# A graph layer on one core: the sums of a round in one stretch, the second layer behind the places, the loop cut ahead of the turns

## The chip, the cores and the metric

The kernel runs on one core of one Trainium2 chip. The metric is the device time of one execution in microseconds (us). About 0.3%, 0.8 us, is what repeated runs can tell from no change.

## The reference

A pre-normalised graph layer with a residual: node features are normalised over their 128 columns, edge features are summed into the node at the edge's end, and a two-layer perceptron is applied to both. There are 12,500 nodes with 128 features, 412,500 edges with 48 features, sorted by their end `dst`; the global vector is one for all nodes, so it is only a bias.

```python
h = jnp.maximum(_layernorm(x, axis=-1), 0.0)
agg = segment_sum(edge_attr_48, dst, num_segments=12500)      # 412500 x 48 -> 12500 x 48
u = graph_globals[zeros]                                      # one row of 64 for all nodes
hid = relu(concatenate([h, agg, u], axis=1) @ W1 + b1)        # 240 -> 256
x = x + hid @ W2 + b2                                         # 256 -> 128
```

All is float32.

## The kernel before

**Rounds.** A loop of 12 rounds handles 1024 nodes and 33,792 edges each; an epilogue does the rest. The nodes of a round are two blocks, A and B, of 512 (128 partitions by 4). The edges of a round are 11 groups of 3072, kept in six *slots*: slots 0 to 3 and 5 hold two groups, slot 4 holds one. A group is loaded as one transfer of 576 KB on SP's queue, for the next round as soon as this round's sums of its slot are done; slots have one buffer each.

**Sums.** Since edges are sorted, a chunk of 768 edges ends in few nodes. `fetch` copies the relative ends of this round's edges from the table `rel` to `rel_i` (L672); `onehots` (VectorE, L686) compares them with a ramp of 28, which makes one-hot matrices `oh`; `sums` (TensorE, L739) multiplies them with the edges, 24 small matmuls a group, into one of two PSUM banks S0 and S1 in turn, and ScalarE copies the result to `ss` (L743). A float32 matmul appears as two records in the profile, so slots 0 to 2 are 288 records and slots 3 to 5 are 240.

**Places.** `places` (VectorE, L692, L705) makes one-hot windows `pl` of 186 nodes, `place` and `place_ends` (TensorE, L761, L726) put the summed chunks at their nodes' columns, in PSUM banks `ax` and `ay`; `sums_out` (ScalarE, L804) copies these to `ags`.

**Normalisation.** `stats` (L768), `variance` (L773 to L778), the root on ScalarE (L779), `shift` (L784, L785) and `norm` (ScalarE, L789, four instructions a block) make `xn` of both blocks. `turn` (L798) transposes it on TensorE, and ScalarE copies it to `ht` (L799).

**Layers.** `layer_x` (L808) and `layer_e` (L813) add the two parts of the first layer in four PSUM banks (PH0 and PH1, PT and PO), each for one block and one half of the hidden 256; `relu` (ScalarE, L818) writes `hid`. The second layer of a round (`second`, TensorE, L834, 16 records a block) is done in the round after, into PH0 and PH1; VectorE adds `xb`, which is x plus the bias, and holds the result in SBUF (L838); `add_b` (L793) makes the `xb` of the new round. Then x of the next round may be loaded, on ScalarE's queue. The held results are stored after the loop.

**Order.** Every engine runs its own instructions in the order in which `body` names them, so an instruction that waits holds back all that is behind it on its engine, the loads on ScalarE's and SP's queues too. `Flow` works out the semaphores. TensorE's loop is cut at another place than that of the other engines: it runs from the operation named in `f.mark` round to the one before it, with one more trip, and the part ahead of the mark on the first trip is skipped. At first trip, where there is no second layer to do, `f.brief` gives one tiny matmul in its place. TensorE's start (the transposes of `dst`, one sum) stands inside this loop, after the first part.

In TensorE's order a round before is: sums 0, 1, 2; second layer of A and of B; sums 3, 4, 5; turns A, B; places; x layer; edge layer. The mark is `su3`, the sums of slot 3.

Of the kernel before, what the change touches and what calls it, by code (L numbers as in the profile page):

```python
# [18 lines left out]
P = 128  # L19
# [35 lines left out]
class Flow:  # L55
# [139 lines left out]
    def run(self):  # L195
# [53 lines left out]
        with nc.Fori(0, hi - lo + 2, 1, engines=[nc.tensor.engine]) as j:  # L249
            with nc.tensor.If(j > 0):  # L250
                for o in own[cut:]:
                    repeat(o, None)
                count("PE")
            with nc.tensor.If(j < 1):
                self.straight([o for o in start if o["eng"] == "PE"])
                ahead("PE")
            with nc.tensor.If(j < hi - lo + 1):
                for brief, some in groupby(own[:cut], lambda o: o["name"] in self.brief):
                    some = list(some)
                    if not brief:  # L260
                        for o in some:
                            repeat(o, None)
                        continue
                    with nc.tensor.If(j > 0):
                        for o in some:
                            repeat(o, None)
                    with nc.tensor.Else():
                        for o in some:
                            repeat(dict(o, emit=self.brief[o["name"]]), None)
        self.straight(end)  # L270
# [151 lines left out]
def kernel(  # L422
# [73 lines left out]
    ot = [const.tile([P, r, D], F32, name=f"ot{k}") for k, r in two]  # L496
    st = [const.tile([P, r, 6], F32, name=f"st{k}") for k, r in two]
    sm = [const.tile([P, 4, r], F32, name=f"sm{k}") for k, r in two]
    sc = [const.tile([P, r], F32, name=f"sc{k}") for k, r in two]
    sh = [const.tile([P, r], F32, name=f"sh{k}") for k, r in two]  # L500

# [107 lines left out]
    def dst_2(b):  # L609
# [4 lines left out]
        dv = df[b % DF].rearrange("c (p t) -> c t p", t=T)  # L614
        rv = rel[:, b * P * T:(b * P + rows) * T].rearrange("p (c t) -> p t c", t=T)
        for t0 in range(0, T, 3):
# [47 lines left out]
    def fetch(j):  # L664

        it = (f.at or 0) + j
        g0, g1 = it * GI + 1, min(NG, (it + 1) * GI + 1)
        m = GI * CG
        blocks = [b for b in range(NB) if b * P < g1 * CG and (b + 1) * P > g0 * CG]
        rv = rel_i.rearrange("p g t -> p (g t)")  # L670

        op("DVE", "fr", ["relz"] + [f"rel{b}.{t0}" for b in blocks for t0 in (0, 3)], ["rel_i"], lambda i: [nc.vector.tensor_scalar(  # L672
            rv, cols(rel, i, lambda i: ((i + j) * GI + 1) * q, m * T), 0.0, None, OP.add)])

# [92 lines left out]
    def stats(k, m=P):  # L767
        op("DVE", f"st{k}", [f"x{k}", f"x{k}t"], [f"st{k}"], lambda i: [nc.vector.bn_stats(st[k][:m, r], xt[k][:m, r]) for r in range(RR[k])])  # L768

    def variance(k, m=P):  # L770
        s = sm[k][:m]
        op("DVE", f"sm{k}.0", [f"st{k}"], [f"sm{k}a"], lambda i: [
            nc.vector.tensor_tensor(s[:, 0:2], st[k][:m, :, 1:3].rearrange("p r c -> p c r"), st[k][:m, :, 4:6].rearrange("p r c -> p c r"), OP.add)])  # L773
        op("DVE", f"sm{k}.1", [f"st{k}"], [f"sm{k}b"], lambda i: [
            nc.vector.tensor_tensor(s[:, 2], st[k][:m, :, 1], st[k][:m, :, 4], OP.subtract)])
        f.chain("DVE", f"sm{k}.2", [f"sm{k}a"], [f"sm{k}b"],
            lambda: nc.vector.tensor_tensor(s[:, 2], s[:, 2], s[:, 2], OP.mult),
            lambda: nc.vector.scalar_tensor_tensor(s[:, 3], s[:, 2], D / 4.0, s[:, 1], OP.mult, OP.add))  # L778
        op("ACT", f"sq{k}", [f"sm{k}b", "eps"], [f"sc{k}"], lambda i: [nc.scalar.activation(sc[k][:m], s[:, 3], AF.Sqrt, bias=eps[:m], scale=1.0 / D)])  # L779

    def shift(k, m=P):
        s = sm[k][:m]
        f.chain("DVE", f"sh{k}", [f"sm{k}a"], [f"sc{k}", f"sh{k}"],
            lambda: nc.vector.reciprocal(sc[k][:m], sc[k][:m]),  # L784
            lambda: nc.vector.scalar_tensor_tensor(sh[k][:m], s[:, 0], -0.5, sc[k][:m], OP.mult, OP.mult))  # L785

    def norm(k, m=P):
        op("ACT", f"xn{k}", [f"x{k}", f"x{k}t", f"sc{k}", f"sh{k}"], [f"xn{k}"], lambda i: [
            nc.scalar.activation(xn[k][:m, r], xt[k][:m, r], AF.Relu, bias=sh[k][:m, r:r + 1], scale=sc[k][:m, r:r + 1]) for r in range(RR[k])])  # L789

# [38 lines left out]

    def second(k, m=P, bk=None, key="PO", keep=None):  # L830

        ov = (po if bk is None else bk)[:, :RR[k] * D].rearrange("p (r d) -> p r d", r=RR[k])
        op("PE", f"w2{k}", [f"hid{k}.{a}" for a in range(NH)] + ["w2"], [key], lambda i: [
            nc.tensor.matmul(ov[:m, r], hid[k][:, a, r, :m], w2[:, a], start=(a == 0), stop=(a == NH - 1)) for r in range(RR[k]) for a in range(NH)])  # L834
        if keep is None:
# [10 lines left out]
    def prologue():  # L846
# [30 lines left out]
        dma("POOL", "lb2", [], ["b2"], b2_sb, b2[None, :].to_broadcast([P, D]))  # L877
        pool("relz", ["relz"], lambda: nc.gpsimd.memset(rel[:, NCH * T:], 0.0))

# [22 lines left out]
        onehot(5, oh[5][:, q:], ["rel0.0", "rel0.3"], rel[:, :q].rearrange("p (g t) -> p g t", g=1))  # L902
        op("PE", "su5", ["oh5", "e5.1"], ["S1"], lambda i: [
# [21 lines left out]
        split("plf", plf, far_, ["off0"], lambda j: off[:, 0:1])  # L925
        op("DVE", "f0", ["rel0.0", "rel0.3"], ["farm"], lambda i: [nc.vector.tensor_reduce(farm, rel[:, :q], AX.X, OP.max, apply_absolute_value=True)])

    def body(it):
        f.at = it

        def add_slots(*some):
            for s in some:
                sums(s)
                if it < NIT - 1:
                    load_e(s, 1)

        keep = lambda i: (i + NIT - 2) % (NIT - 1)
        farthest()
        fetch(1)
        add_slots(0, 1)  # L940
# [36 lines left out]
        layers(layer_e)  # L977
        layers(relu)

    def epilogue():  # L980
# [5 lines left out]
        stats(Z, m)  # L986
        variance(Z, m)
        shift(Z, m)
        norm(Z, m)
# [41 lines left out]
    f.order((0, NIT - 1))  # L1031
    f.mark = "su3"
    f.brief = {f"w2{k}": lambda i, k=k: [nc.tensor.matmul(ph[k][:, 0:1], hid[k][:, 0, 0], w2[:, 0, 0:1], start=True, stop=True)] for k in (A, B)}
    tc.mark_branch_hint_location("skip", engines=[ET.PE, ET.DVE])
# [35 lines left out]
```

## Time and profile before

| | |
|---|---|
| median of 3 runs | 261.3 us (260.92 to 261.72) |
| profiled execution | 261.09 us, span of its instructions 259.3 us |
| TensorE busy | 237.5 us, 92% |
| VectorE busy | 237.4 us, 92% |
| ScalarE busy | 128.6 us, 50% |
| transfers | 94.33 MB, mean 364 GB/s |

The profile is of one execution. Busy time is the time in which an engine had at least one instruction under way. In lists of instructions, L739 is a line of the kernel, `s<-e,oh` is what it writes and reads, x288 is how many follow each other; PE is TensorE, PEld its weight load, DVE VectorE, ACT ScalarE, SP the engine that issues most transfers; a q behind an engine is its queue of issues. In the page's slices the span is cut into 40 equal parts, a digit is a share in tenths. "issue" as the cause of a stop means that the engine waited for nothing that the profile shows.

### The profile page before, as it was taken

What the parts mean: (1) busy time and instruction counts of PE and PEld (TensorE: products, weight loads), DVE (VectorE), ACT (ScalarE), POOL (GpSimd) and SP (SyncE); (2) the same over time, 40 slices, a digit from 0 to 9 for tenths busy, and PEclk for the clock granted to TensorE, in tenths of its full rate; (3) what the DMA queues carried; (4) which work ended last, traced back from release to release, by engine and by line L of the source; (5) the groups of instructions that cost most, each with busy time, mean ns of one, the idle gap of its engine ahead of it and who ended that gap; (6) DMA issues with size and microseconds to landing.
All of it is one profiled execution on the core that took longest, in us unless ns stands there. A gap on an engine that the chain in (4) does not pass through costs nothing.

```text
span 259.3 us, 17135 instructions
## 1 busy us (share of the span) xinstructions
PE 237.5 (92%) x7539; PEld 185.9 (72%) x7540; DVE 237.4 (92%) x643; ACT 128.6 (50%) x326; POOL 9.1 (4%) x23
## 2 busy tenths in 40 slices
PE   0864889999999999999999999999999999999990
PEld 0854765976967958949859769679589498597680
DVE  5799999999999999999999999999999999999640
ACT  4630454644645536646546446455366465564520
POOL 8200020000000000000000000000000000000000
PEclk9997599999999999999999999999999999999999
DMA  6999999999999999999999999999999999959951
GB/s 215 285 380 388 364 389 391 390 392 390 390 392 390 391 392 390 391 392 390 390 393 390 393 389 391 392 385 388 393 382 389 393 385 390 393 210 350 364 223 65
DMA packets 79012, 94.33 MB, mean 364 GB/s; under 512 B 3227, under 2 KB 72189, under 8 KB 78998
## 3 DMA queue, kind: packets, MB, share of 16 engines
q1 hardware_dynamic: 75398, 87.63, 94.6%
q10 hardware_dynamic: 3312, 6.03, 6.1%
q0 software_dynamic: 288, 0.49, 0.7%
q8 instruction: 7, 0.11, 0.2%
q14 instruction: 7, 0.06, 0.1%
HBM read 87.75 MB, written 6.40 MB: 363 GB/s over the span
## 4 chain that ended last, share of the span: by engine, by line
PE 86%; DVE 6%; DMA 2%; issue 2%; ACT 1%; SPq 0%; DVEq 0%
PE s L739 26%; PE ph L834 17%; PE ph L808 9%; PE ax L761 7%; PE ph L813 5%; PE po L808 4%; PE pt L808 4%; PE pt L813 4%; DVE oh L686 3%; PE pt L798 3%; DMA holda<-in_dst_dram 2%; PE po L798 2%; PE ax L726 2%; DVE pl L692 1%; PE s L992 1%
## 5 line engine op out<-in xcount | busy, mean ns | idle before, releaser
L686 DVE TENSOR_TENSOR oh<-iota_v,rel_i 128x1344 f32<-128x1344 f32 (+1 forms) x78 | 108.6, 1435 | 0.0
L739 PEld LDWEIGHTS s<-e,oh 128*28 128x28 f32 x6336 | 73.0, 110 | 18.3 <-issue 15.9
L739 PE MATMUL s<-e,oh 128*28 128x48 f32 x6336 | 76.9, 211 | 8.1 <-issue 4.6
L743 ACT COPY ss<-s 128x96 f32<-128x96 f32 (+1 forms) x72 | 16.5, 230 | 26.6 <-PE s L739 26.5
L692 DVE TENSOR_SCALAR pl<-iota_w,off_i 128x186 f32<-128x186 f32 x117 | 27.6, 312 | 0.4
L789 ACT ACTIVATE xna<-xa,sha,sca 128x128 f32<-128x128 f32 x48 | 19.8, 482 | 15.9 <-DVE sha L785 15.9
L818 ACT ACTIVATE hida<-ph,bias 128x512 f32<-128x512 f32 x12 | 8.2, 687 | 38.3 <-PE ph L813 38.3
L834 PE MATMUL ph<-w,hida 128*128 128x128 f32 x192 | 24.6, 281 | 0.0
L834 PE MATMUL ph<-w,hidb 128*128 128x128 f32 x192 | 23.4, 275 | 0.0
L834 PEld LDWEIGHTS ph<-w,hida 128*128 128x128 f32 x192 | 22.3, 191 | 0.8
L834 PEld LDWEIGHTS ph<-w,hidb 128*128 128x128 f32 x192 | 22.4, 192 | 0.0
L789 ACT ACTIVATE xnb<-xb,shb,scb 128x128 f32<-128x128 f32 x48 | 19.6, 480 | 0.0
L761 PE MATMUL ax<-pl,ss 128*48 128x186 f32 (+1 forms) x120 | 19.4, 309 | 0.0
L761 PE MATMUL ay<-pl,ss 128*48 128x186 f32 (+1 forms) x120 | 19.4, 309 | 0.0
L761 PEld LDWEIGHTS ax<-pl,ss 128*48 128x48 f32 x120 | 13.8, 123 | 4.7 <-issue 2.0
L799 ACT COPY hta<-pt 128x512 f32<-128x512 f32 x12 | 7.0, 587 | 15.2 <-DVE xbb L793 14.9
L761 PEld LDWEIGHTS ay<-pl,ss 128*48 128x48 f32 x120 | 13.8, 123 | 0.0
L813 PE MATMUL ph<-ags,w1a 48*128 48x512 f32 x48 | 13.5, 641 | 0.0
L808 PE MATMUL ph<-hta,w1h 128*128 128x512 f32 x24 | 13.5, 645 | 0.0
L808 PE MATMUL ph<-htb,w1h 128*128 128x512 f32 x24 | 12.3, 592 | 0.0
L808 PE MATMUL pt<-hta,w1h 128*128 128x512 f32 x24 | 12.3, 592 | 0.0
L808 PE MATMUL po<-htb,w1h 128*128 128x512 f32 x24 | 12.3, 592 | 0.0
(162 smaller groups left out, 334.7 us busy)
## 6 DMA issues: line engine op xcount, KB each, us to landing
e<-in_edge_attr_dram SPq DMA_DIRECT2D x133, 576.0 KB, 9.3
xa<-in_x_dram ACTq DMA_DIRECT2D x11, 256.0 KB, 5.4
xb<-in_x_dram ACTq DMA_DIRECT2D x11, 256.0 KB, 5.5
out_dram<-holda SPq DMA_DIRECT2D x11, 256.0 KB, 3.5
out_dram<-holdb SPq DMA_DIRECT2D x11, 256.0 KB, 3.5
holda<-in_dst_dram SPq DMA_DIRECT2D x4, 384.0 KB, 5.7
e<-in_edge_attr_dram SPq DMA_DIRECT2D x1, 720.0 KB, 6.3
xa<-in_x_dram SPq DMA_DIRECT2D x1, 256.0 KB, 8.8
```

Of the source, the lines that this page charges most:

```text
L686: op("DVE", f"oh{name}", reads + ["iota_v"], [f"oh{name}"], lambda i: [nc.vector.tensor_tensor(ov, iota_v[:, None, None, :].to_broadcast([ ...
L692: nc.vector.tensor_scalar(out[:, j], iota_w, o[j], None, OP.is_equal) for j in range(len(o))])
L739: nc.tensor.matmul(S[k][NV * c:NV * c + V, j * DE:(j + 1) * DE], o[:, (j * CG + c) * T + t], ev[:, j * CG + c, t * DE:(t + 1) * DE], start ...
L743: op("ACT", f"ss{name}", [f"S{k}"], [f"ss{name}"], lambda i: [nc.scalar.copy(sv.rearrange("p j d -> p (j d)"), S[k][:, :m * DE])])
L761: out.append(nc.tensor.matmul(agg[bk][h:h + DE, at:at + w], sv[:, j], pv[:, j, frm:frm + w], start=bk in fresh and bk not in seen, stop=Tr ...
L789: nc.scalar.activation(xn[k][:m, r], xt[k][:m, r], AF.Relu, bias=sh[k][:m, r:r + 1], scale=sc[k][:m, r:r + 1]) for r in range(RR[k])])
L798: op("PE", f"tu{k}", [f"xn{k}", "ident"], [key], lambda i: [nc.tensor.transpose(pv[:, r, :m], xn[k][:m, r], ident[:m, :m]) for r in range( ...
L799: op(eng, f"hT{k}", [key], [f"hT{k}"], lambda i: [copy(hT[k][:, :, :m], pv[:, :, :m])])
L808: nc.tensor.matmul(o, w1h[:, a * P:(a + 1) * P], hT[k][:, :, :m], start=first, stop=False, skip_group_check=True)])
L813: nc.tensor.matmul(o, w1a[h:h + DE, a * P:(a + 1) * P], ag[k // 2][h:h + DE, :, :m], start=False, stop=True, skip_group_check=True)])
L818: nc.scalar.activation(hid[k][:, a, :, :m], o, AF.Relu, bias=bias[:, a:a + 1])])
L834: nc.tensor.matmul(ov[:m, r], hid[k][:, a, r, :m], w2[:, a], start=(a == 0), stop=(a == NH - 1)) for r in range(RR[k]) for a in range(NH)])
```

## The change

- In TensorE's order a round becomes: sums 0 to 5; places; second layer of A, and of B without its last quarter (`second_begun`, 28 records in all); turns A, B; the last quarter of B's second layer (4 records); x layer and edge layer, now with the banks PT and PO first and PH0 and PH1 last. The mark is `tu0`, the turn of A.
- The variances, roots and shifts of A and B are worked out together: one chain of VectorE instructions and one root on ScalarE for eight columns. The root stands behind the copy of slot 5's sums on ScalarE.
- The load of x of A stands behind the copies of the sums on ScalarE's queue, that of B behind `keep_ends`; VectorE's one-hots, held results and `add_b` are put in a new order.
- TensorE's start stands in a loop of two trips that does nothing on the first. In the first round only A's brief matmul is done, and B's last quarter runs on a hidden layer that is set to zero.
- `rel` is kept with the six edges of a partition apart (`[P, T, C]`), so its filling writes contiguous rows and `fetch` reads with a stride.
- In the start, slot 2's one-hots go behind the offsets of the other chunks.

```diff
             with nc.tensor.If(j > 0):
                 for o in own[cut:]:
                     repeat(o, None)
                 count("PE")
-            with nc.tensor.If(j < 1):
-                self.straight([o for o in start if o["eng"] == "PE"])
-                ahead("PE")
+            with nc.tensor.Else():
+                with nc.Fori(0, 2, 1, engines=[nc.tensor.engine]) as k:
+                    with nc.tensor.If(k > 0):
+                        self.straight([o for o in start if o["eng"] == "PE"])
+                        ahead("PE")
...
-    rel = const.tile([P, ((NIT + 1) * GI + 1) * q], F32)
+    rel = const.tile([P, T, ((NIT + 1) * GI + 1) * CG], F32)
...
-            rv, cols(rel, i, lambda i: ((i + j) * GI + 1) * q, m * T), 0.0, None, OP.add)])
+            rv, (rel[:, :, at(i):at(i) + m] if isinstance(i, int) else rel[:, :, ds(at(i), m)]).rearrange("p t c -> p c t"),
+            0.0, None, OP.add)])
...
-    middle = [(a, k) + v for a, bs in enumerate(((("PH0", ph[0]), ("PH1", ph[1])), (("PT", pt), ("PO", po)))) for k, v in enumerate(bs)]
+    middle = [(a, k) + v for a, bs in ((1, (("PT", pt), ("PO", po))), (0, (("PH0", ph[0]), ("PH1", ph[1])))) for k, v in enumerate(bs)]
...
+    def second_begun(k, bk, key, n):
+        ov = bk.rearrange("p (r d) -> p r d", r=R)
+        op("PE", f"w2{k}a", [f"hid{k}.{a}" for a in range(NH)] + ["w2"], [key], lambda i: [
+            nc.tensor.matmul(ov[:, r], hid[k][:, a, r], w2[:, a], start=(a == 0), stop=(a == NH - 1)) for r in range(n) for a in range(NH)])
...
+            if k == B:
+                blank("hidl", "hid1.1", hid[k][:, :, R - 1], [P, NH, P])
...
-        onehots(2)
         op("DVE", "bj", ["PH1", "b1"], ["bias"], lambda i: [nc.vector.tensor_tensor(bias, ph[1][:, NG:NG + NH], b1_sb, OP.add)])
         dst_3(ph[1], "PH1", range(1, NB))
+        onehots(2)
...
-        farthest()
-        fetch(1)
         add_slots(0, 1)
-        for k in (A, B):
-            stats(k)
-            variance(k)
-        add_slots(2)
+        stats(A)
+        farthest()
+        fetch(1)
         onehots(0)
-        shift(A)
-        shift(B)
+        add_slots(2, 3)
+        stats(B)
+        variance(0, (A, B))
         onehots(1)
+        add_slots(4, 5)
+        root(0)
+        shift(0)
         onehots(2)
+        onehots(3)
         norm(A)
         norm(B)
-        for k in (A, B):
-            second(k, P, ph[k], f"PH{k}", keep)
-            add_b(k)
-
-        add_slots(3, 4, 5)
-        if it < NIT - 1:
-            load_x(A, lambda i: (i + 1) % NIT * IN)
-            load_x(B, lambda i: (i + 1) % NIT * IN + BN)
-        for s in (3, 4, 5):
-            onehots(s)
-        turn(A)
-        turn(B, P, po, "PO")
         place(0, (0, 1))
         for s in (1, 2, 3, 4):
             place(s)
         place_ends((0, 1))
+        second(A, P, ph[A], "PH0", keep)
+        add_b(A)
+        for s in (4, 5):
+            onehots(s)
+        second_begun(B, ph[B], "PH1", R - 1)
         sums_out(A)
         sums_out(B)
+        if it < NIT - 1:
+            load_x(A, lambda i: (i + 1) % NIT * IN)
+        turn(A)
+        turn(B, P, po, "PO")
+        second(B, P, ph[B], "PH1", keep, R - 1)
+        add_b(B)
         keep_ends()
+        if it < NIT - 1:
+            load_x(B, lambda i: (i + 1) % NIT * IN + BN)
         places_far()
...
-    f.mark = "su3"
-    f.brief = {f"w2{k}": lambda i, k=k: [... one tiny matmul ...] for k in (A, B)}
+    f.mark = "tu0"
+    f.brief = {"w20": lambda i: [... one tiny matmul ...], "w21a": None}
```

More of the change, by code (lines that the diff above doesn't have):

```diff
@@ L496 @@
     ot = [const.tile([P, r, D], F32, name=f"ot{k}") for k, r in two]
[L497 to L500, printed above, removed]
+    one = (("ab", 2 * R), ("r", RZ))
+    st = [const.tile([P, r, 6], F32, name=f"st{k}") for k, r in one]
+    sm = [const.tile([P, 4, r], F32, name=f"sm{k}") for k, r in one]
+    sc = [const.tile([P, r], F32, name=f"sc{k}") for k, r in one]
+    sh = [const.tile([P, r], F32, name=f"sh{k}") for k, r in one]
     hold = [const.tile([P, max(NIT - 1, n) * R * D], F32, name=f"hold{k}") for k, n in (("a", -(-(NB + DF) * CE // (R * D))), ("b", 0))]
@@ L614, in dst_2 @@
         dv = df[b % DF].rearrange("c (p t) -> c t p", t=T)
-        rv = rel[:, b * P * T:(b * P + rows) * T].rearrange("p (c t) -> p t c", t=T)
+        rv = rel[:, :, b * P:b * P + rows]
         for t0 in range(0, T, 3):
@@ L767, in stats @@
     def stats(k, m=P):
[L768 to L776, printed above, removed]
+        c = k % 2 * R
@@ new lines, in stats, with variance @@
+        op("DVE", f"st{k}", [f"x{k}", f"x{k}t"], [f"st{k}"], lambda i: [nc.vector.bn_stats(st[k // 2][:m, c + r], xt[k][:m, r]) for r in range(RR[k])])
+    def variance(n, ks, m=P):
+        s, v = sm[n][:m], st[n][:m]
+        op("DVE", f"sm{n}.0", [f"st{k}" for k in ks], [f"sm{n}a"], lambda i: [
+            nc.vector.tensor_tensor(s[:, 0:2], v[:, :, 1:3].rearrange("p r c -> p c r"), v[:, :, 4:6].rearrange("p r c -> p c r"), OP.add)])
+        op("DVE", f"sm{n}.1", [f"st{k}" for k in ks], [f"sm{n}b"], lambda i: [
+            nc.vector.tensor_tensor(s[:, 2], v[:, :, 1], v[:, :, 4], OP.subtract)])
+        f.chain("DVE", f"sm{n}.2", [f"sm{n}a"], [f"sm{n}b"],
@@ L777, in variance, with root @@
             lambda: nc.vector.tensor_tensor(s[:, 2], s[:, 2], s[:, 2], OP.mult),
             lambda: nc.vector.scalar_tensor_tensor(s[:, 3], s[:, 2], D / 4.0, s[:, 1], OP.mult, OP.add))
[L779 to L785, printed above, removed]
+    def root(n, m=P):
+        op("ACT", f"sq{n}", [f"sm{n}b", "eps"], [f"sc{n}"], lambda i: [
+            nc.scalar.activation(sc[n][:m], sm[n][:m, 3], AF.Sqrt, bias=eps[:m], scale=1.0 / D)])
@@ L787, in norm, with shift @@
+    def shift(n, m=P):
+        s = sm[n][:m]
+        f.chain("DVE", f"sh{n}", [f"sm{n}a"], [f"sc{n}", f"sh{n}"],
+            lambda: nc.vector.reciprocal(sc[n][:m], sc[n][:m]),
+            lambda: nc.vector.scalar_tensor_tensor(sh[n][:m], s[:, 0], -0.5, sc[n][:m], OP.mult, OP.mult))
     def norm(k, m=P):
-        op("ACT", f"xn{k}", [f"x{k}", f"x{k}t", f"sc{k}", f"sh{k}"], [f"xn{k}"], lambda i: [
-            nc.scalar.activation(xn[k][:m, r], xt[k][:m, r], AF.Relu, bias=sh[k][:m, r:r + 1], scale=sc[k][:m, r:r + 1]) for r in range(RR[k])])
+        n, c = k // 2, k % 2 * R
+        op("ACT", f"xn{k}", [f"x{k}", f"x{k}t", f"sc{n}", f"sh{n}"], [f"xn{k}"], lambda i: [
+            nc.scalar.activation(xn[k][:m, r], xt[k][:m, r], AF.Relu, bias=sh[n][:m, c + r:c + r + 1], scale=sc[n][:m, c + r:c + r + 1])
+            for r in range(RR[k])])
@@ L828, in layers, with second @@
             fn(f"{k}.{a}", key, bk.rearrange("p (r c) -> p r c", r=R), k, a)
-    def second(k, m=P, bk=None, key="PO", keep=None):
+    def second_begun(k, bk, key, n):
+        ov = bk.rearrange("p (r d) -> p r d", r=R)
+        op("PE", f"w2{k}a", [f"hid{k}.{a}" for a in range(NH)] + ["w2"], [key], lambda i: [
+            nc.tensor.matmul(ov[:, r], hid[k][:, a, r], w2[:, a], start=(a == 0), stop=(a == NH - 1)) for r in range(n) for a in range(NH)])
+    def second(k, m=P, bk=None, key="PO", keep=None, begun=0):
         ov = (po if bk is None else bk)[:, :RR[k] * D].rearrange("p (r d) -> p r d", r=RR[k])
         op("PE", f"w2{k}", [f"hid{k}.{a}" for a in range(NH)] + ["w2"], [key], lambda i: [
-            nc.tensor.matmul(ov[:m, r], hid[k][:, a, r, :m], w2[:, a], start=(a == 0), stop=(a == NH - 1)) for r in range(RR[k]) for a in range(NH)])
+            nc.tensor.matmul(ov[:m, r], hid[k][:, a, r, :m], w2[:, a], start=(a == 0), stop=(a == NH - 1)) for r in range(begun, RR[k]) for a in range(NH)])
         if keep is None:
@@ L877, in prologue @@
         dma("POOL", "lb2", [], ["b2"], b2_sb, b2[None, :].to_broadcast([P, D]))
-        pool("relz", ["relz"], lambda: nc.gpsimd.memset(rel[:, NCH * T:], 0.0))
+        pool("relz", ["relz"], lambda: nc.gpsimd.memset(rel[:, :, NCH:], 0.0))
         op("DVE", "c0", [], ["eps", "zero", "worst1", "worst2"], lambda i: [
@@ L986, in epilogue @@
         stats(Z, m)
-        variance(Z, m)
-        shift(Z, m)
+        variance(1, (Z,), m)
+        root(1, m)
+        shift(1, m)
         norm(Z, m)
@@ L1031 @@
     f.order((0, NIT - 1))
-    f.mark = "su3"
-    f.brief = {f"w2{k}": lambda i, k=k: [nc.tensor.matmul(ph[k][:, 0:1], hid[k][:, 0, 0], w2[:, 0, 0:1], start=True, stop=True)] for k in (A, B)}
+    f.mark = "tu0"
+    f.brief = {"w20": lambda i: [nc.tensor.matmul(ph[A][:, 0:1], hid[A][:, 0, 0], w2[:, 0, 0:1], start=True, stop=True)], "w21a": None}
     tc.mark_branch_hint_location("skip", engines=[ET.PE, ET.DVE])
```

12 lines of the change are left out of this document (7 added, 5 removed).

## The prediction

> **What bounds the kernel now.** I read the page first, its busy shares and the 40 slices of part 2.
>
> ```profile
> PE 237.5 (92%) x7539; PEld 185.9 (72%) x7540; DVE 237.4 (92%) x643; ACT 128.6 (50%) x326; POOL 9.1 (4%) x23
> ...
> PEclk9997599999999999999999999999999999999999
> DMA  6999999999999999999999999999999999959951
> GB/s 215 285 380 388 364 389 391 390 392 390 390 392 390 391 392 390 391 392 390 390 393 390 393 389 391 392 385 388 393 382 389 393 385 390 393 210 350 364 223 65
> ```
>
> TensorE, VectorE and the transfers are all full. Next the chain that ended last, over one round of the loop (rows of the places left out, the last two rows are the round after and the end of the loop):
>
> ```profile
> 98.05 3.20 PE s L739 x288
> 101.25 3.77 PE ph L834 x32
> 105.02 2.74 PE s L739 x240
> 107.76 0.59 PE pt L798 x4
> 108.35 0.44 PE po L798 x4
> 108.78 0.29 PE ax L761
> ...
> 110.66 1.91 PE ph L808 x4
> 112.58 0.86 PE pt L808 x2
> 113.44 0.86 PE po L808 x2
> 114.29 1.06 PE ph L813 x4
> ...
> 116.21 0.80 PE s L739 x61
> ```
>
> It is TensorE without a hole: sums 3.20, second layer 3.77, sums 2.74, turns 1.02, places 1.88 (108.78 to 110.66), x layer 3.63, edge layer 1.92; 18.16 a round. So TensorE's order is what the change must shorten. But the transfers stand close behind. A round moves 11 groups of 576 KB and two blocks of x of 256 KB, 7.01 MB; at the slices' 391 GB/s that is 17.93 us. Whether 391 is a ceiling or only what the kernel asks for, the issues tell:
>
> ```profile
> 208.23 18.54 SPq L540 DMA_DIRECT2D e<-in_edge_attr_dram  x12
> 25.96 0.39 SPq L540 DMA_DIRECT2D e<-in_edge_attr_dram  x1
> e<-in_edge_attr_dram SPq DMA_DIRECT2D x1, 576.0 KB, 7.5
> 221.62 1.87 SPq L540 DMA_DIRECT2D e<-in_edge_attr_dram  x1
> e<-in_edge_attr_dram SPq DMA_DIRECT2D x1, 576.0 KB, 9.2
> ```
>
> SP's issues follow each other almost without a break (about 1.5 us each, the time of 576 KB at 391 GB/s), so the queue is backed up. The last group of slot 5 for round 0 lands at 25.96 + 7.5 = 33.5, the one for the last round at 221.62 + 9.2 = 230.8: 197.3 us for 11 rounds, 17.93 each. Two counts agree, so I take 391 for a ceiling. TensorE at 18.16 falls behind it by 0.23 a round, and slot 5 is read late in the round, so today nothing waits.
>
> The third thing is the first round, at 18 to 35 us, where part 2 shows TensorE's clock at 0.5 to 0.7:
>
> ```profile
> 18.70 1.62 PE L739 MATMUL s<-e,oh 128*28 128x48 f32 x84 [2.55 <-DVE vv L629]
> 21.03 2.27 PE L739 MATMUL s<-e,oh 128*28 128x48 f32 x127 [0.72 <-issue]
> 27.22 1.81 PE L739 MATMUL s<-e,oh 128*28 128x48 f32 x77 [3.91 <-issue]
> 35.03 0.66 PE L798 MATMUL pt<-ident,xna 128*128 128x128 f32 x4
> q8 instruction: 1, 0.02, 5.7%
> ```
>
> TensorE stops after 84 matmuls and again exactly 127 later, for 0.72 and 3.91 us, "issue", with nothing to wait for. 127 matmuls and their 127 weight loads are 254 instructions; queue 8 carried one packet of 0.02 MB of instructions in the window 24.9 to 26.0 (the last row), just before TensorE went on. So the first passage through TensorE's code is paced by loading it: 6.19 us (21.03 to 27.22) for a block of 127 matmuls, through the same busy transfer engines, and the next block only asked for once one is entered. From 33 to 236 us the transfer view lists no instruction packet: later rounds find their code loaded.
>
> **The change, part by part.** Call E the end of slot 5's sums, R the start of a round's sums.
>
> TensorE's round. Work is the same; what goes is switching between shapes of the array. The first turns cost 0.59 against 0.44 for the second group, the first x pair 1.05 (1.91 - 0.86) against 0.86, the first edge pair 1.06 against 0.86 for the other (up to 116.21); so a switch is 0.07 to 0.2. Now there are seven (edge-sums, sums-layer, layer-sums, sums-turns, turns-places, places-x, x-edge), afterwards four (edge-sums, sums-places, places-layer, x-edge). I take three at 0.1: 18.16 - 0.28 = 17.88 a round (ends 17.55 and 17.95). From E to the next R: places 1.88, 28 of the layer's 32 records 3.25, turns 0.9, the last 4 records 0.45, x 3.5, edge 1.92: 11.9. Before it was 8.45, since the second layer stood ahead of slots 3 to 5.
>
> Slot 5's data. Reading slot 5 at R + 5.9 instead of R + 9.7 takes 3.8 us from what its last load had in hand. At the end of the loop: landing 230.8, 0.6 for the group's 48 matmuls and the start, 11.9: the loop cannot end before 243.3. In the profile it ends, with the first sums of the epilogue, here:
>
> ```profile
> 243.34 1.75 PE s L992 x72
> ```
>
> So by the transfers alone the change is worth nothing: 0.28 a round is saved on TensorE, and the ceiling takes it back through the second layer that now lies behind the last landing.
>
> The first round. The loop is turned: its top is 28 matmuls instead of 292, and all 528 sums now lie one after the other in the first passage. 528 at 127 a block means four boundaries. 292 - 28 moves 264 matmuls, 528 instructions, two blocks and 16 instructions; so the boundary that stood after sum 84 stands after 92, then 219, 346 and 473, in slot 5. Before, the passage crossed two and then jumped back to the code of slots 3 to 5, already there at 29.9. The two-trip loop around TensorE's start visits the code behind it early, which can fetch the block behind the first boundary before the transfers are busy; I take that block as free. First sums: VectorE's offsets go ahead of slot 2's one-hots, 1.47 us earlier, so 18.70 becomes 17.2, and the first boundary is entered at 18.0. Three more blocks at 6.19: 36.6. Then 55 matmuls, 0.6 at the rate of 288 in 3.20, twice that at half clock: E of round 0 at 37.4, though the data is there at 33.5. Bounds: no cost if the blocks come ahead (E 34.3, by the data), and 2 us more if the first is not free either.
>
> VectorE. One variance chain and one shift instead of two:
>
> ```profile
> 100.73 0.17 DVE L773 TENSOR_TENSOR smb<-stb 128x8 f32<-128x8 f32 x1
> 101.29 1.55 DVE L686 TENSOR_TENSOR oh<-iota_v,rel_i 128x1344 f32<-128x1344 f32 x1
> 98.16 0.30 DVE L672 TENSOR_SCALAR rel_i<-rel 128x264 f32 x1
> ```
>
> 100.73 to 101.29: 0.56 less in 18.16, besides two small instructions of the shift. The fetch of rel (L672) reads with a stride now: between nothing and its own 0.30 again. VectorE needs some 17.5 to 17.8 and is no bound, but it waits anew: the shift follows the square root, which on ScalarE follows slot 5's copy, and behind the shift stand all later one-hots, the second layer's sums and add_b.
>
> ScalarE after E, the new tight path:
>
> ```profile
> 107.83 0.24 ACT L743 COPY ss<-s 128x96 f32<-128x96 f32 x1 [0.88 <-PE s L739]
> 100.43 0.30 ACT L779 ACTIVATE sca<-sma,eps 128x4 f32<-128x4 f32 x1
> 103.16 1.65 ACT L789 ACTIVATE xna<-xa,sha,sca 128x128 f32<-128x128 f32 x4 [1.33 <-DVE sha L785]
> 106.26 0.68 DVE L838 TENSOR_TENSOR holda<-ph,xba 128x512 f32 x1
> 108.10 0.34 ACTq L540 DMA_DIRECT2D xa<-in_x_dram  x1
> 109.41 0.59 ACT L799 COPY hta<-pt 128x512 f32<-128x512 f32 x1 [1.35 <-DVE xbb L793]
> L692 DVE TENSOR_SCALAR pl<-iota_w,off_i 128x186 f32<-128x186 f32 x117 | 27.6, 312 | 0.4
> xa<-in_x_dram ACTq DMA_DIRECT2D x11, 256.0 KB, 5.4
> ```
>
> Copy, root and shift end at E + 1.0; two norms to 4.1; two copies of the sums (0.6 each) to 5.3. Meanwhile VectorE does two one-hots (3.0), from E + 0.9 to 3.9, the held sum behind the second layer's first half (E + 4.0), and add_b, about as long as it, to E + 5.4. Only then does ScalarE issue x of block A (0.34), and the turned copy, queued behind that issue, ends at E + 6.4. TensorE comes to the x layer at 1.88 + 3.25 + 0.9 + 0.45 = 6.5. It just fits: no cost, with 0.1 to spare. x of A lands 5.4 after its issue, at 10.8. VectorE goes on with slots 4 and 5 (2.2), the held sum and add_b of B (1.4, to 9.0) and the windows (27.6 in 12 rounds, 2.3 each, and the ends), and reads A at about 12. B is issued at 9.0; by A's row it lands at 14.4, and is read behind slot 0's one-hots at about 15. Both are hidden by these; without the cover VectorE would stop for the difference, and it has 0.1 to 0.4 a round to spare. B's issue makes ScalarE wait up to 9.0, and behind it stand the four activations of the layer, wanted at about 11. SP's loads come in a closer burst, into a queue that is backed up anyway. POOL's memset is six strided pieces at the start, ACT's extra blank lies where ScalarE idles; both nothing.
>
> Sum: 37.4 + 11 x 17.88 + 11.9 = 246.0 against 243.34, 2.6 us more; the epilogue is unchanged. The profiled execution took 261.09 (span 259.3), so 263.7; the median of the runs is 0.2 above it: 263.9.
>
> The Trainium skill, page "Runtime: NRT & Kernel Launch", section "Instruction fetch mechanics", says that instructions come in 16 KiB blocks of 256, that the next is fetched while the current one runs, and that crossing a boundary is mostly hidden. The 3.91 us stop speaks against "mostly hidden" while the transfer engines are full; block size and the quiet after 33 us agree with the page. By that rule the first passage costs nothing, which is the first rival.
>
> **The rivals.** *The code loading is hidden* (the two-trip loop brings more than one block ahead). Then E of round 0 is 34.3, TensorE would be at 34.3 + 196.7 + 11.9 = 242.9, and the landing at 230.8 holds it to 243.3: 261.3, no change. For it: a visit of the code before the transfers fill. Against: after each of the two stops, one block came and no more.
>
> *391 GB/s is no ceiling*, or the switches are worth the upper end: then 34.3 + 11 x 17.55 + 11.9 = 239.3, 4 us less, 257.3; it decides from a landing of the last slot 5 before 230. Against it: 17.93 by two counts, and no slice of the loop above 393.
>
> *The ScalarE path is late.* If the turned copy comes 0.2 us after TensorE, each round has it: 11 x 0.2 on top, 266.1. For it: the 0.1 in hand.
>
> **How the numbers follow.** Slow first passage 0.48, hidden loading 0.26, no ceiling 0.12, late ScalarE path on top 0.14. The forecast is the first, 263.9; by itself 262.4 to 265.3 (first boundary 1 us either way, 17.85 to 17.95 a round). The range takes in the no-change case and the late path: 260.7 to 266.2. About 0.3%, 0.8 us, is what a measurement can tell. Slower is the late path and nearly all of the forecast, 0.61; same is the hidden loading, 0.25; faster is the missing ceiling with a fringe of the others, 0.14.
>
> **What would show it.** Right: TensorE stops marked "issue" of some microseconds inside the first 528 sums, first turns near 40 us instead of 35.03; later turns 17.9 apart; SP's issues still unbroken. The landing ceiling: waits of the last sums on e in every round. The ScalarE path: x layer (L808) waiting for hta. Wrong if the first turns come by 38, or rounds are 17.6 apart with the last slot 5 landing well before 230.8.

## The result and the profile after

The changed kernel took 263.71 us (median of 14 runs, 262.61 to 264.7), the one before 261.37 on the same chip (14 runs): ratio 1.0075, 95% interval 1.0053 to 1.0097. The forecast was 263.9. The profiled execution took 263.96 us with a span of 262.2, against a span of 259.3 before: 2.9 us more.

First the busy shares and the slices of the page of the changed kernel, to be held against those of before:

```profile
PE 237.4 (91%) x7541; PEld 187.0 (71%) x7542; DVE 232.7 (89%) x571; ACT 122.9 (47%) x315; POOL 7.6 (3%) x23
...
PEclk9975579999999999999999999999999999999996
...
GB/s 209 293 390 388 368 387 387 174 354 392 388 381 392 392 390 394 390 390 394 390 392 392 391 392 390 391 393 390 391 391 390 392 392 391 393 288 343 367 218 64
```

TensorE's busy time is the same to 0.1 us, VectorE's is 4.7 less, and the run is longer: no engine's work explains it. What is new is in the slices: the transfers drop to 174 GB/s in slice 8 (46 to 52 us), and TensorE's clock is at 0.5 to 0.7 in four slices of the start instead of two. So the first round comes first. The timeline of TensorE there (start, duration, shape, count, in brackets the idle time ahead and what ended it):

```profile
14.81 0.71 PE L745 MATMUL s<-e,oh 128*28 128x48 f32 x48 [0.71 <-DMA e<-in_edge_attr_dram]
...
19.26 1.18 PE L745 MATMUL s<-e,oh 128*28 128x48 f32 x48 [0.23 <-DMA e<-in_edge_attr_dram]
21.86 0.81 PE L745 MATMUL s<-e,oh 128*28 128x48 f32 x26 [1.42 <-DMA e<-in_edge_attr_dram]
23.96 1.66 PE L745 MATMUL s<-e,oh 128*28 128x48 f32 x70 [1.29 <-issue]
26.19 1.18 PE L745 MATMUL s<-e,oh 128*28 128x48 f32 x48 [0.58 <-DMA e<-in_edge_attr_dram]
27.60 0.52 PE L745 MATMUL s<-e,oh 128*28 128x48 f32 x10 [0.23 <-DMA e<-in_edge_attr_dram]
29.81 2.77 PE L745 MATMUL s<-e,oh 128*28 128x48 f32 x127 [1.69 <-issue]
36.54 1.34 PE L745 MATMUL s<-e,oh 128*28 128x48 f32 x55 [3.96 <-issue]
37.81 0.54 PE L767 MATMUL ax<-pl,ss 128*48 128x186 f32 x1
```

Count the matmul records up to each stop marked "issue" (two of the four rows of 48 are left out above): 4 x 48 + 26 = 218, then 70 + 48 + 10 = 128 more (346), then 127 (473), then the last 55. These are the second, third and fourth boundary of the prediction (219, 346, 473); at the first, 92, nothing stops. The places begin at 37.81; the forecast was 37.4.

Next the chain that ended last, over a round (rows of the places left out):

```profile
85.40 5.80 PE s L745 x528
...
93.08 1.98 PE ph L851 x16
...
96.40 0.44 PE pt L810 x4
...
97.27 0.45 PE ph L851 x4
97.72 1.01 PE pt L820 x2
...
103.22 0.79 PE s L745 x61
```

From sums to sums 103.22 - 85.40 = 17.82 (18.16 before). Sums 5.80 (before 3.20 + 2.74), places 1.88 (91.20 to 93.08, as before), second layer and turns 4.64 (93.08 to 97.72; before 3.77 + 1.02), x and edge layer 5.50 (before 5.55). Last, the starts of the sums of some rounds and the last round's data, in the timeline and, in the second fence, the list of issues (KB, us from issue to landing):

```profile
49.73 0.46 PE L745 MATMUL s<-e,oh 128*28 128x48 f32 x24
67.52 0.48 PE L745 MATMUL s<-e,oh 128*28 128x48 f32 x25
210.32 0.37 PE L745 MATMUL s<-e,oh 128*28 128x48 f32 x16
228.25 0.46 PE L745 MATMUL s<-e,oh 128*28 128x48 f32 x24
223.25 1.77 SPq L544 DMA_DIRECT2D e<-in_edge_attr_dram  x1
234.21 0.36 PE L767 MATMUL ax<-pl,ss 128*48 128x186 f32 x1
246.14 1.03 PE L1015 MATMUL s<-e,oh 128*28 128x48 f32 x56
```

```profile
e<-in_edge_attr_dram SPq DMA_DIRECT2D x1, 576.0 KB, 10.3
```

An early round takes 67.52 - 49.73 = 17.79, a late one 228.25 - 210.32 = 17.93. The last slot 5 lands at 223.25 + 10.3 = 233.5, its places start 0.7 later, and 11.93 after that the loop ends, at 246.14. Here is the whole difference, the epilogue being the same:

- sums of the first round end at 37.81 instead of 35.03: +2.78
- from there to the next sums 11.92 (49.73 - 37.81) instead of 8.45, since the second layer now lies behind: +3.47
- eleven rounds in 246.14 - 49.73 = 196.4, 17.86 each, instead of 11 x 18.16 = 199.8: -3.4

Together +2.9. The rounds do get shorter, by just about what the moved second layer costs once; the longer first passage is what remains.

### The profile page after: what moved, and what is told of

It reads as the page before. It is cut to its first block, busy times and chain, and to the rows that moved or that the text cites. A ratio compares the mean times of both kernels' runs of the same rounds, so it can differ in the third digit from the quotient of the medians.

```text
span 262.2 us, 17089 instructions
## 1 busy us (share of the span) xinstructions
PE 237.4 (91%) x7541; PEld 187.0 (71%) x7542; DVE 232.7 (89%) x571; ACT 122.9 (47%) x315; POOL 7.6 (3%) x23
## 4 chain that ended last, share of the span: by engine, by line
PE 83%; SPq 6%; DMA 4%; issue 3%; ACT 2%; DVE 0%; ACTq 0%
PE s L745 26%; PE ph L851 12%; PE ph L820 8%; PE ax L767 6%; SPq L544 6%; PE ph L845 6%; PE pt L825 5%; PE pt L820 5%; PE ph L825 4%; PE po L820 4%; DMA e<-in_edge_attr_dram 4%; PE po L810 2%; PE pt L810 2%; PE ax L732 1%; PE s L1015 1%
## 5 line engine op out<-in xcount | busy, mean ns | idle before, releaser
L692 DVE TENSOR_TENSOR oh<-iota_v,rel_i 128x1344 f32<-128x1344 f32 (+1 forms) x78 | 109.8, 1436 | 0.4
L745 PEld LDWEIGHTS s<-e,oh 128*28 128x28 f32 x6336 | 74.2, 111 | 21.6 <-issue 18.8
L830 ACT ACTIVATE hida<-pt,bias 128x512 f32<-128x512 f32 x12 | 8.2, 687 | 50.2 <-PE pt L825 50.2
L800 ACT ACTIVATE xna<-xa,shab,scab 128x128 f32<-128x128 f32 x48 | 19.8, 482 | 5.7 <-DVE shab L795 5.7
L800 ACT ACTIVATE xnb<-xb,shab,scab 128x128 f32<-128x128 f32 x48 | 19.6, 479 | 0.0
L845 PE MATMUL ph<-w,hidb 128*128 128x128 f32 x132 | 16.5, 275 | 0.0
L845 PEld LDWEIGHTS ph<-w,hidb 128*128 128x128 f32 x132 | 15.6, 192 | 0.0
L820 PE MATMUL pt<-hta,w1h 128*128 128x512 f32 x24 | 13.5, 643 | 1.0 <-ACT hta L811 1.0
L825 PE MATMUL pt<-ags,w1a 48*128 48x512 f32 x24 | 13.5, 641 | 0.0
L825 PE MATMUL po<-ags,w1a 48*128 48x512 f32 x24 | 13.5, 641 | 0.0
```

The lines of the kernel that those rows point to most:

```text
L692: op("DVE", f"oh{name}", reads + ["iota_v"], [f"oh{name}"], lambda i: [nc.vector.tensor_tensor(ov, iota_v[:, None, None, :].to_broadcast([ ...
L745: nc.tensor.matmul(S[k][NV * c:NV * c + V, j * DE:(j + 1) * DE], o[:, (j * CG + c) * T + t], ev[:, j * CG + c, t * DE:(t + 1) * DE], start ...
L820: nc.tensor.matmul(o, w1h[:, a * P:(a + 1) * P], hT[k][:, :, :m], start=first, stop=False, skip_group_check=True)])
L825: nc.tensor.matmul(o, w1a[h:h + DE, a * P:(a + 1) * P], ag[k // 2][h:h + DE, :, :m], start=False, stop=True, skip_group_check=True)])
L845: nc.tensor.matmul(ov[:, r], hid[k][:, a, r], w2[:, a], start=(a == 0), stop=(a == NH - 1)) for r in range(n) for a in range(NH)])
```

## The experiments

The theory: the passage through code not yet loaded decides the sign, and behind it stands the transfers' ceiling. The rivals: the first passage is paced by data or clock; the ceiling isn't one; something else of the change (VectorE's order, one variance for both) moves the time.

**Undo the turning of the loop.** The loop's cut goes back to the sums of slot 3; the order in a round stays. (Not shown below: the hidden layers are set to zero whole, as the first round now does its second layer in full.)

```
-    f.mark = "tu0"
-    f.brief = {"w20": lambda i: [... one tiny matmul ...], "w21a": None}
+    f.mark = "su3"
+    f.brief = {}
```

> The new kernel with one thing undone: TensorE's loop is cut at the sums of slot 3 again, as before, so the first passage crosses only the code of slots 0 to 2 and then goes back to the loop's top. (The hidden layers are zeroed whole, and the first round does its second layer in full, 3.2 us on TensorE that lie beside ScalarE's path.) Theory, code loading: the first places move from 37.8 to 34.5 to 35.5 us, set by the landing of the last slot 5 at about 33; rounds stay 17.8 and turn to 17.93 as the transfers hold them; the loop ends at 243.3 to 243.9, total 261.1 to 261.9, 2 to 2.5 less than the changed kernel. Rival, the new order itself (ScalarE behind slot 5's copy, loads of x late): no difference to the changed kernel, 263.5 to 264.

271.55 us, ratio 1.0384 (1.0328 to 1.044). The timeline of TensorE in the first round, and the chain in a later one:

```profile
...
29.39 5.77 PE L745 MATMUL s<-e,oh 128*28 128x48 f32 x352 [2.93 <-issue]
35.09 0.36 PE L767 MATMUL ax<-pl,ss 128*48 128x186 f32 x1
```

```profile
104.86 3.20 PE s L745 x288
108.06 0.44 issue
108.51 2.80 PE s L745 x238
```

With one large stop in the sums instead of three, the places begin at 35.09, 2.7 us earlier, as the theory has it, although TensorE did its first matmul only at 14.05 (5.17 in the changed kernel). The total missed: the cut now lies between the sums of two slots, and the loop's turn stops TensorE for 0.44 in every round; rounds take 18.40 instead of 17.80, and the x layer of round 0 came 2.5 us late. So the first step is borne out, but this edit can't give the time without the loop's turn.

**The side edits alone.** The order of before, with the new layout of rel, one variance for both blocks and one shift.

```
-        for k in (A, B):
-            stats(k)
-            variance(k)
+        stats(A)
+        stats(B)
+        variance(0, (A, B))
+        root(0)
...
-        shift(A)
-        shift(B)
+        shift(0)
```

> The kernel before with only the side edits: one variance chain and shift for both blocks, rel with the edges apart, slot 2's one-hots behind the offsets in the start; TensorE's order and cut as before. Theory, TensorE's order is the bound: rounds stay 18.16, VectorE gets 0.6 to 0.9 us of idle time a round, total 261.0 to 261.6, the same. Rival, VectorE (as busy as TensorE, 92%) holds the rounds: 0.6 us less a round, 254 to 256.

261.04 us, ratio 0.9974 (0.9942 to 1.0006); rounds 18.16. The window by engine in the middle of the loop (length, then busy time of TensorE, its weight loads, VectorE, ScalarE and GpSimd):

```profile
100.00:120.00 20.00, 20.00 (x712) 15.80 (x700) 19.02 (x45) 10.73 (x29) 0.00 (x0) 1.00 1.08 391
```

VectorE (the third pair) is busy for 19.02 of 20, against 19.45 in the same window of before, and TensorE for 20.00 in both: VectorE is near full without being the bound.

**The early visit taken away.** TensorE's start is no longer inside a two-trip loop.

```
-            with nc.tensor.Else():
-                with nc.Fori(0, 2, 1, engines=[nc.tensor.engine]) as k:
-                    with nc.tensor.If(k > 0):
-                        self.straight([o for o in start if o["eng"] == "PE"])
-                        ahead("PE")
+            with nc.tensor.If(j < 1):
+                self.straight([o for o in start if o["eng"] == "PE"])
+                ahead("PE")
```

> The changed kernel without the two-trip loop around TensorE's start: the code behind the start isn't visited early. Theory, one block is fetched ahead, and only once the block before it is entered: the block behind the first boundary (after some 92 sums) comes a little later or in time, the three others 6.2 us apart as now; first places at 37.8 to 40, total 263.6 to 266. Rival, the early visit has no part in it: 263.7, first places at 37.8, and the first instruction packet comes at another time with no effect.

264.73 us, ratio 1.0108 (1.0054 to 1.0163); the interval overlaps that of the changed kernel, so its time alone decides nothing. The timeline does (first and last of the four stops marked "issue"; the two between are of 2.50 and 2.89 us):

```profile
18.73 2.28 PE L743 MATMUL s<-e,oh 128*28 128x48 f32 x98 [1.43 <-issue]
...
37.29 1.33 PE L743 MATMUL s<-e,oh 128*28 128x48 f32 x53 [3.62 <-issue]
38.55 0.55 PE L765 MATMUL ax<-pl,ss 128*48 128x186 f32 x1
```

A fourth stop appears, after 94 sums, where the prediction had the free boundary; the places begin 0.74 later. Queue 8, which carries the code, says why: in the changed kernel its first packet lands at 6.92 us, without the visit at 17.31, and TensorE goes on at 18.73.

**The early visit stretched**, so that its jump lands one block further on (over the start and the sums of slots 0 and 1), or two (up to slot 3).

```
-            with nc.tensor.Else():
+            with nc.tensor.If(j < hi - lo + 1):
+                far = [o["name"] for o in own].index("su2")   # second kernel: "su4"
                 with nc.Fori(0, 2, 1, engines=[nc.tensor.engine]) as k:
                     with nc.tensor.If(k > 0):
-                        self.straight([o for o in start if o["eng"] == "PE"])
-                        ahead("PE")
-            with nc.tensor.If(j < hi - lo + 1):
-                for brief, some in groupby(own[:cut], lambda o: o["name"] in self.brief):
+                        with nc.tensor.If(j < 1):
+                            self.straight([o for o in start if o["eng"] == "PE"])
+                            ahead("PE")
+                        for o in own[:far]:
+                            repeat(o, None)
+                for brief, some in groupby(own[far:cut], lambda o: o["name"] in self.brief):
```

> As visit_further, but on its first trip the stretched loop jumps only over the start and the sums of slots 0 and 1, so it lands in the block next to those already there instead of two beyond. The loop turn inside the sums costs its 0.2 a round as in visit_further (17.98). Theory, code loading: that block and the one behind it are asked for before the first sums; of the three steps of 6.2 us after 17.6 only the later ones are left, first places at 34.8 to 36.5 (37.8 in the changed kernel, 41.7 in visit_further); total 262.5 to 264.5 with the slower rounds. Rival, the first places are late for another reason than code: 37.5 or later, as the work is the same.

> The changed kernel, order and cut as it has them, with the two-trip loop stretched: on its first trip TensorE jumps over its start and over the sums of slots 0 to 3, so that it visits the code of slots 4 and 5 at the very start and that block, and perhaps the one behind it, is loaded while TensorE waits for dst. (In later rounds the inner loop is passed too; a turn of a loop inside the sums may cost up to 0.4 a round, as cut_at_su3 showed.) Theory, code loading in the first passage: one or two of the three 6.2 us steps go, first places at 34 to 35.5 instead of 37.8, the last slot 5 lands at 230.5 to 231.5 instead of 233.5; loop end 243.2 to 244.5 if the rounds keep 17.8, total 261 to 262.3; with 0.4 a round on top up to 265, but first places early all the same. Rival, the late first places come from ScalarE, VectorE or the half clock: first places stay at 37.5 to 38.

Both missed, in direction: 270.21 us, ratio 1.0319 (1.0254 to 1.0383) for one block, 268.86, ratio 1.0292 (1.0255 to 1.0329) for two. The timeline with one block:

```profile
17.79 1.21 PE L748 MATMUL s<-e,oh 128*28 128x48 f32 x92
22.24 2.86 PE L748 MATMUL s<-e,oh 128*28 128x48 f32 x126 [3.23 <-issue]
28.65 2.78 PE L748 MATMUL s<-e,oh 128*28 128x48 f32 x128 [3.55 <-issue]
35.05 2.77 PE L748 MATMUL s<-e,oh 128*28 128x48 f32 x127 [3.62 <-issue]
41.24 0.99 PE L748 MATMUL s<-e,oh 128*28 128x48 f32 x55 [3.41 <-issue]
42.16 0.55 PE L770 MATMUL ax<-pl,ss 128*48 128x186 f32 x1
```

Four stops after 92, 218, 346 and 473 sums, 6.2 to 6.4 us from start to start. The last slot 5 of round 0 had landed at 33.0, against 32.8 in the changed kernel, and the sums are the same; still the places begin at 42.16 (41.70 with two blocks). This speaks against pacing by data. What the visit brought, the rows of queue 8 say, 2 to 50 us, of the changed kernel and of the visit with one block (packets, MB, share):

```profile
q8 instruction: 5, 0.08, 0.7%
```

```profile
q8 instruction: 8, 0.13, 1.2%
```

Eight packets of instructions instead of five, with two blocks as well. Three land before 15 us, TensorE's first matmul comes at 9.47 us (8.77 with two blocks) instead of 5.17, and still each of the four boundaries has its stop: what the jump brought did not serve the passage. That the same blocks were loaded twice is likely, but not shown, since the records do not say which code a packet holds.

**Less to transfer.** The changed kernel, but slot 4 is loaded once and not in each round (its later sums are made from old data). A second and a third kernel do the same to the cut at slot 3 and to the longer visit.

```
-                if it < NIT - 1:
+                if it < NIT - 1 and s != 4:
```

> The changed kernel, but slot 4's group is never loaded again in the rounds (9% fewer bytes of edges; its sums run on the first round's data). Nothing else differs, so the code and the first passage should be as in the changed kernel. Theory, the transfers hold the rounds from the seventh on: all eleven rounds are 17.80 and the last five no longer 17.93, which is 0.6 us; the last slot 5 lands microseconds before it is read. Rival, the rounds of 17.93 come from ScalarE or VectorE: they stay.

> As cut_at_su3, but slot 4's group is never loaded again in the rounds (one of 11 groups, 9% of the edges' bytes; its sums run on the first round's data). Theory, 391 GB/s is a ceiling that holds the new order: rounds are 17.8 to the end, loop ends 242.0 to 242.7, total 259.9 to 260.7, about 1 less than cut_at_su3. Rival, no ceiling: the same as cut_at_su3 within 0.3.

> As visit_further, but slot 4's group is never loaded again in the rounds (9% fewer bytes; its sums run on the first round's data). Theory, the transfer ceiling of 391 GB/s holds the new order once the first passage is quick: rounds at TensorE's own pace to the end, total 0.5 to 1.2 below visit_further. If visit_further is held by TensorE (rounds of 18.0 or more), no difference within 0.3.

273.31 us (ratio 1.0429, 1.0391 to 1.0468), 271.14 (1.0364, 1.032 to 1.0408) and 277.09 (1.0606, 1.056 to 1.0652). All three are late for a reason that the edit brings along: TensorE now waits ahead of the loop for slot 4's landing (13.21, 7.96 and 12.00 us), so the times tell nothing; and the two others, bound by TensorE in their rounds (18.38 to 18.44, and 17.98), don't tell of the ceiling at all. The first does. TensorE's timeline, its first round and two later ones:

```profile
30.75 3.85 PE L745 MATMUL s<-e,oh 128*28 128x48 f32 x218 [13.21 <-DMA e<-in_edge_attr_dram]
35.64 1.59 PE L745 MATMUL s<-e,oh 128*28 128x48 f32 x128 [1.04 <-issue]
43.36 2.78 PE L745 MATMUL s<-e,oh 128*28 128x48 f32 x127 [6.14 <-issue]
47.90 0.80 PE L745 MATMUL s<-e,oh 128*28 128x48 f32 x55 [1.76 <-issue]
48.63 0.36 PE L767 MATMUL ax<-pl,ss 128*48 128x186 f32 x1
...
220.66 0.55 PE L745 MATMUL s<-e,oh 128*28 128x48 f32 x32
...
238.45 0.76 PE L745 MATMUL s<-e,oh 128*28 128x48 f32 x52
```

The late round takes 238.45 - 220.66 = 17.79, like the early ones; with the full load it was 17.93. So the transfers hold the late rounds, by 0.14 each. And the first passage still takes 17.9 us (30.75 to 48.63), though its last data had landed at 33.3: the stops come with all data there. Nor does the clock make them: it was granted in full (1.00) from 30 to 40 us, and the longest stop begins in this time, at 37.2.

**The gain without the price.** If the switches between shapes are what shortens the round, one can be had without moving the second layer behind slot 5. The kernel of the side edits, with the turns moved right behind the second layer; the loop's cut stays ahead of slot 3's sums. So that the turns find `xn` ready, the statistics come first in a round and the norms ahead of the sums of slot 2 (not shown below).

```
         for k in (A, B):
             second(k, P, ph[k], f"PH{k}", keep)
             add_b(k)
+        turn(A)
+        turn(B, P, po, "PO")
         add_slots(3, 4, 5)
...
-        turn(A)
-        turn(B, P, po, "PO")
```

> Another order: the old one with one variance chain, the statistics first in a round, and the turns moved between the second layer and the sums of slot 3 (both use the whole array, so a switch of shape goes: six instead of seven); behind slot 5's sums only places and the first layer are left, 7.4 us instead of 11.9. Theory: rounds 18.05 (18.16 less 0.1), slot 5 is read late as before, so no ceiling; first places at 35 to 36.5 (in the first round the turns wait for xn), loop end at 35.7 + 11 x 18.05 + 7.4 = 241.7, total 259 to 260.5, faster by 0.4 to 0.8%. Rival: xn isn't ready for the turns (ScalarE, VectorE), rounds of 18.3 or more, 262 and up.

260.19 us, ratio 0.9939 (0.9914 to 0.9963): faster than both kernels. Its chain:

```profile
97.86 3.20 PE s L743 x288
...
104.83 0.44 PE pt L808 x4
...
105.70 2.74 PE s L743 x240
...
115.87 2.13 PE s L743 x187
```

18.01 a round; the first turns cost 0.44 instead of 0.59 behind sums, and that is the whole gain: 0.15 x 11 = 1.65, less 0.28 for a later first round (places at 36.33 instead of 36.05) makes 1.37. The loop ends at 241.88 instead of 243.27.

## Why the prediction was right

**First passage.** "E of round 0 at 37.4": 37.81, with three stops at the boundaries named and the first one free. What the stops wait for stands in the trace's records of queue 8. In the changed kernel its packets of 16 KB start at 21.54, 27.31 and 34.01 us and land at 22.53, 28.34 and 35.12; TensorE goes on at 23.96, 29.81 and 36.54, each time 1.4 to 1.5 us behind a landing. The view of transfers, in a window of 26.9 to 28 us, has the second of them:

```profile
q8 instruction: 1, 0.02, 5.8%
```

In the other kernels too, each stop of over half a microsecond marked "issue" inside the first round's sums ends 1.2 to 1.5 us behind the landing of such a packet. The taking away and the stretching of the visit moved E with the number of stops (37.81 with three, 38.55, 41.70 and 42.16 with four), and not with the data. The rule of the Trainium skill (page "Runtime: NRT & Kernel Launch", section "Instruction fetch mechanics") that a boundary is mostly hidden doesn't hold in this first passage: stops of 1.29, 1.69 and 3.96 us. The first rival falls with it.

That the sum came out so near is in part luck. The first sums came at 14.81 and not at 17.2, then waited for their data, and passed the first boundary at 17.1 instead of 18.0; the three steps behind it took 6.8, 5.9 and 6.7 us instead of 6.19 each. The two misses cancel.

The reason that the prediction gave for 6.19 us a block, the busy transfer engines, was not tested by itself, but the changed kernel with less to load speaks for it. There TensorE passed the first boundary at 32.6, with the transfers nearly still (18 GB/s from 32 to 34 us): the next packet started 0.5 us later, and its block could be entered after 3.1 us. At the next two boundaries, 35.64 and 43.36, with the transfers between 233 and 384 GB/s again, the packets started 5.5 and 2.3 us later. In the changed kernel, with the transfers full, it was 3.3 to 4.4 us. Each packet itself took about 1 us. So a block came fast where the transfer engines were almost idle, but the wait ahead of a packet does not follow the rate alone.

**Rounds.** "Three at 0.1", 17.88: TensorE needs 17.79, the saving being 0.37. In the round shown it is 0.34: 0.14 in the sums (5.94 to 5.80, one break less), 0.15 in second layer and turns, 0.05 in x and edge layer. The estimate was a little small. The late rounds are held to 17.93 by the transfers, as the two counts of before said; so the mean came out at 17.86. That this falls on the 17.88 of the forecast is luck: a saving larger than forecast and a hold that the forecast did not have inside the rounds make up for each other.

**The end.** "11.9": 11.93. But the place of the ceiling was off. The prediction had the landing at 230.8, so that the loop "cannot end before 243.3", and let TensorE be later than that by the first passage. In fact both bind one behind the other: slots were freed late in the first round, and SP stood still for it, where the prediction had expected "SP's issues still unbroken". The waits of SP's queue from 40 to 60 us (in the kernel before, the same view is empty):

```profile
SPq L544 <- PE s L745: 8.2, 1, 8.2
```

At 174 GB/s (slice 8, 46 to 52 us) instead of some 390, six us lose about 3.3 us of transfer time (6 x 217 / 391). The shorter rounds then catch up with the delayed transfers around round 7, and the last landing is 233.5, 2.7 later than before. "Waits of the last sums on e in every round" came true only from round 7 on, and so short (0.11 to 0.16 between the starts of the last sum of slot 4 and the first of slot 5, where neighbours are 0.01 apart, worked out from the records) that the view of waits lists none. In the kernel with less to load this gap is gone.

**ScalarE's path.** "It just fits: no cost" is almost so. The x layer starts 6.43 to 6.48 us after the first places in every round from 1 on (6.5 forecast), and for its matmuls the view of waits lists one wait for the turned copy in the whole run, in round 0:

```profile
PE pt L820 <- ACT hta L811: 1.0, 1, 1.0
```

But the path binds in the later rounds too. ScalarE's issue of x and the turned copy, in the round shown:

```profile
96.55 0.38 ACTq L544 DMA_DIRECT2D xa<-in_x_dram  x1
96.97 0.58 ACT L811 COPY hta<-pt 128x512 f32<-128x512 f32 x1 [0.54 <-PE pt L810]
```

(The view names the turn as what ended the idle time, since it does not count an issue as work.) By the records, the copy starts 0.04 us behind the end of this issue in each of the eleven rounds that have it, and the first weight load of the x layer starts 0.05 behind the end of the copy in all twelve (97.60 behind 97.55), just as in round 0, where the wait is listed. In the last round there is no issue; the copy comes 0.06 or more earlier behind the turns, and the x layer follows the second layer 0.06 sooner (0.60 instead of 0.66 to 0.69 from its last matmul to the second one of the x layer). So the third rival, 0.2 us in each round, is right in kind and wrong in size: some 0.06 in ten rounds, 0.6 us in all (an estimate from these starts, no run took the path away), more than made up for by the larger saving.

**No ceiling**, the second rival, is out by the run with less to load. **VectorE**: the strided fetch costs 0.38 to 0.42 instead of 0.30, inside the bounds, and hidden, as the side edits alone show.

## What to carry to other kernels

Ahead of turning a loop or merging stretches, count the instructions of the first passage: each block of short matmuls that has to be loaded can stop the engine, and the price doesn't shrink with more rounds. A move that shortens every round but puts work behind the last landing pays for that work once; if the transfers are near their ceiling, the shorter round can't be cashed in. Look for the part of the move (here, one change of shape) that has neither price.

## What the runs showed of the hardware that was not expected

- A loop's turn inside a run of short matmuls costs a stop of 0.44 us (rounds 0.6 longer); ahead of the turns, or between second layer and sums, no row shows it.
- A jump far ahead into code not yet loaded did worse than none: eight packets of instructions instead of five, the first places at 41.70 and 42.16, against 38.55 with no early visit and 37.81 with the short one.
- In the changed kernel blocks follow each other 5.9 to 6.8 us apart, in the stretched visit with one block 6.2 to 6.4. Of it 2.8 are the matmuls of a block where the clock was granted at 0.50, twice what 127 take in a later round (3.20 for 288); a packet takes about 1, and TensorE goes on 1.2 to 1.5 after it has landed. Ahead of a packet pass 3.3 to 4.4 us with the transfers full, 0.5 with the transfers nearly still; what sets this wait stays open.
- A stall of TensorE of some us early in the run came back 180 us later, as a landing 2.7 us later, through slots freed late in a queue that had no slack.
